# A graph layer's edge counts in 7 places a dense tile instead of 11, three lists to a PSUM bank

## The chip, the cores and the metric

The kernel runs on one core of one Trainium2 chip. The metric is the device time of one execution in microseconds; the time before is the median of three runs, 1500.9 us (1500.37 to 1501.51).

## The reference

6250 nodes of 256 numbers, 200000 edges. Three branches read the normalised input: a graph convolution, a mixer (linear attention with two layer norms and a gelu network), and, on the sum of the two, a mixture of eight experts with a capacity of tokens each.

```python
xn = layernorm(x)
# graph convolution, self loops added
h = xn @ W;  norm = dinv[src] * dinv[dst]
gnn = relu(segment_sum(h[src] * norm[:, None], dst) + b)
# mixer: q, k = elu(.) + 1; linear attention over all nodes, 8 heads
t  = (q @ kv) / (q @ ksum + 1e-6)
x1 = layer_norm(t + xn, ln1_g, ln1_b)
mix = layer_norm(gelu(x1 @ W1.T + b1) @ W2.T + b2 + x1, ln2_g, ln2_b)
x = x + gnn + mix
# experts: gate, argmax, place in the expert's buffer, two layers, times the probability
idx = argmax(softmax(layernorm(x) @ gate_w + gate_b))
x = x + ffn_of_experts(layernorm(x), idx)
```

The edges are sorted by their destination `dst`.

## The kernel before

The nodes are 49 tiles of 128. A first stage (to about 247 us) normalises x, makes q, k and v, sums the attention's `kv`, and leaves the rows `h` of all nodes twice: in SBUF as `tab` and in DRAM as `g_dram`. The stage that is changed follows, to about 1130 us. The experts run behind it, to the end.

**Dense tiles.** 32 of the 49 destination tiles (`ND = 32`) get their sum as a full product: a matrix A of edge counts (source node by destination node) times `tab`, 49 products of 128x128 by 128x512 into the bank `ps_d` (L1199), after an identity product (L1195, the self loops) and a product with left-over rows (L1196). A is counted by TensorE: the edges of a tile's 128 destinations are cut into 44 lists (`NG`), 40 of three destinations and 4 of two. Of each list VectorE makes two one-hot matrices (`onehots`, L1134): `lo` (128 wide, the source within its tile) and `hi` (148 wide, source tile times destination in the list). Their product, `lo` by `hi` (L1177), is 49 x 3 = 147 columns of counts. Two lists share a PSUM bank `bp` (pool of 2); ScalarE evicts it as uint8 into `A` (L1181; L1184 for the two-node lists). Later ScalarE widens `A`, 4 or 5 of the 49 blocks at a time, to `A_r` (L1165, 2 buffers), the weights of the products at L1199.

`dense()` is a generator that yields once a place; a tile has `half = NG // 4` = 11 places. In place p the tile u−1 gets the products of share p (places 1 to 10), the one-hots of place p+1 are made (`lo` and `hi` in 3 buffers), the next share is widened, and `counted` issues the counts of place p−1 with their evictions: four lists, two banks. In place 0 there are no products of L1199. In the last place `put_sum` (ScalarE, L1121) and `put_rest` (VectorE, L1126) take `ps_d` away.

**Gathered tiles.** The other 17 tiles are summed over gathered rows: 33 products each (`EB`), 561 in all (`NGT`). For each, GpSimd starts an indirect DMA of 128 rows into `gt` (L1230; 9 buffers, 7 ahead), VectorE makes a one-hot `oh` for every two (L1245, made four products ahead, 3 buffers), TensorE multiplies into `ps` (L1256). Each tile has an identity product first and, two products later, one with `ohg` (L1255; `ohg` from L1242). `gather()` yields after each product.

**Rounds.** Everything else of the 49 tiles goes by pairs: 25 rounds. A step of a round is a function, and `at(k, f)` puts it into place k of a plan; round a starts at `SLOTS_A_ROUND * a`, 14 places. In the order of a round: `scaled`, `attend` (two halves, L1453, a bank each) and `attended` (VectorE, L1464 and L1466), `mix_stats`, `mix_norm` (L1379), `mix_turn` and `mix_turned` (L1488), `first` (L1496), `gelu` (ScalarE, two instructions, L1504), `second` (L1512, L1514), `mixed` (L1523); second statistics, `gain`, `shift`, `joined`; then for an earlier pair `add_bias`, `to_slot` (L1390), statistics, `slot_turn`, `slot_turned`, `gate` (L1422), `put_logits` (L1427), and for every two pairs a `routing` that is walked in ten steps and ends in scatters to `xbuf` (GpSimd, L1337). `start_roots` and `end_roots` make the inverse roots of a round's variances on VectorE. All PSUM banks of the rounds come from one pool of three (`bank()`, tile `mm`).

The engines run their own instructions in the order in which this driver issues them:

```python
g_rate = (NGT + LAG - 0.8 * ahead) / (n_dense - G_EARLY - ahead)
...
for n in range(n_dense + 1):
    ...
    step("d")
    while counts["s"] < min(s_end, (n - S_LATE) * S_RATE) and step("s"):
        pass
    while counts["g"] < 0.8 * min(n + 1, ahead) + max(0, n + 1 - ahead) * g_rate and step("g"):
        pass
```

So one place is: the dense tile's share, one place of the plan of rounds (`S_RATE` = 1.0104), and about 1.6 gathered products.

## Time and profile before

| | |
|---|---|
| median of 3 runs | 1500.9 us (1500.37 to 1501.51) |
| profiled execution, its own time | 1500.01 us |
| its span | 1498.2 us |
| mean granted TensorE clock | 0.979 |
| first stage (0 to 247 us), TensorE busy | 215.75 us |
| dense, gathered and rounds (247 to 1130 us), TensorE busy | 845.85 of 883 us |
| the end of the rounds (1130 to 1190 us), TensorE busy | 50.32 of 60 us |
| experts (1190 us to the end), TensorE busy | 285.75 of 308 us |

PE is TensorE's matrix products and PEld its weight loads, DVE is VectorE, ACT ScalarE, POOL GpSimd, SP the engine that only starts DMAs. A group of instructions is shown by its line and operation, with the tiles it writes and reads (`out<-in`), its number, its busy time and the mean of one in ns, and the idle time of its engine just before it with what ended that. A wait is shown as the line that waited, the line that it waited for, the sum in us, how often, and the longest.

### The profile page before, as it was taken

What the parts mean: (1) busy time and instruction counts of PE and PEld (TensorE: products, weight loads), DVE (VectorE), ACT (ScalarE), POOL (GpSimd) and SP (SyncE); (2) the same over time, 40 slices, a digit from 0 to 9 for tenths busy, and PEclk for the clock granted to TensorE, in tenths of its full rate; (3) what the DMA queues carried; (4) which work ended last, traced back from release to release, by engine and by line L of the source; (5) the groups of instructions that cost most, each with busy time, mean ns of one, the idle gap of its engine ahead of it and who ended that gap; (6) DMA issues with size and microseconds to landing.
All of it is one profiled execution on the core that took longest, in us unless ns stands there. A gap on an engine that the chain in (4) does not pass through costs nothing. (4 is left out here: it accounts for less than half of the span.)

```text
span 1498.2 us, 22383 instructions
## 1 busy us (share of the span) xinstructions
PE 1397.7 (93%) x7002; PEld 1020.9 (68%) x7002; DVE 1004.2 (67%) x3435; ACT 900.1 (60%) x2051; POOL 745.3 (50%) x725
## 2 busy tenths in 40 slices
PE   5998997999998999999999989999997999999996
PEld 2665664777776777777776767767775767766854
DVE  6787696678887887878888878888865322222322
ACT  2776564677776777677776767777674333333321
POOL 0101542777776677777766677777661201111111
PEclk9999998999999999999999999999998999999998
DMA  8438675877787777877777777777765343333130
GB/s 266 144 124 275 195 233 172 225 198 201 188 219 207 180 201 211 223 200 214 204 202 205 196 192 202 186 209 210 182 170 171 120 149 110 127 129 132 47 109 11
DMA packets 173459, 267.52 MB, mean 179 GB/s; under 512 B 26409, under 2 KB 73984, under 8 KB 173318
## 3 DMA queue, kind: packets, MB, share of 16 engines
q0 software_dynamic: 89168, 166.39, 42.7%
q1 hardware_dynamic: 83268, 98.39, 19.9%
q10 hardware_dynamic: 882, 1.05, 0.3%
q8 instruction: 65, 1.06, 0.3%
q14 instruction: 76, 0.62, 0.1%
HBM read 208.05 MB, written 60.39 MB: 179 GB/s over the span
## 5 line engine op out<-in xcount | busy, mean ns | idle before, releaser
L1230 POOL DMA_INDIRECT gt<-g_dram,idxc x561 | 592.9, 1057 | 217.1 <-PE ps L1256 79.7
L1199 PE MATMUL ps_d<-tab,A_r 128*128 128x512 f32 x1568 | 425.8, 401 | 10.2 <-ACT A_r L1165 9.9
L1199 PEld LDWEIGHTS ps_d<-tab,A_r 128*128 128x128 f32 x1568 | 292.7, 190 | 88.6 <-ACT A_r L1165 26.5
L1181 ACT CAST A<-bp 128x294 uint8<-128x294 f32 x640 | 237.2, 430 | 186.9 <-PE bp L1177 185.4
L1165 ACT CAST A_r<-A 128x640 fp32r<-128x640 uint8 (+1 forms) x320 | 230.7, 723 | 6.6 <-PE ps_d L1199 5.0
L1256 PE MATMUL ps<-gt,oh 128*128 128x512 f32 x561 | 220.4, 451 | 2.5 <-DVE oh L1245 2.5
L1177 PE MATMUL bp<-hi,lo 128*128 128x147 bf16 x1408 | 187.3, 264 | 22.0 <-DVE hi L1134 13.1
L1177 PEld LDWEIGHTS <-lo 128*128 128x128 bf16 x1408 | 105.0, 105 | 123.0 <-issue 49.3
L1838 POOL DMA_INDIRECT out<-rep,who x43 | 42.5, 989 | 279.4 <-DVE rep L1835 225.5
L1804 PE MATMUL hpf<-xet,w1e 128*128 128x128 f32 (+3 forms) x576 | 159.2, 434 | 8.2 <-ACTq L1916 3.5
L1134 DVE TENSOR_TENSOR lo<-rowb,two 128x512 bf16<-128x512 bf16 x352 | 147.4, 419 | 21.0 <-PE bp L1177 13.6
L1134 DVE TENSOR_TENSOR hi<-hib,two 128x592 bf16<-128x592 bf16 x352 | 161.5, 459 | 0.0
L1814 PE MATMUL ypf<-w2e,hm 128*128 128x256 f32 (+1 forms) x688 | 151.4, 379 | 0.0
L1814 PEld LDWEIGHTS ypf<-w2e,hm 128*128 128x128 f32 (+1 forms) x688 | 128.8, 188 | 21.6 <-issue 2.6
L1245 DVE TENSOR_TENSOR oh<-rowb,rel 128x256 fp32r<-128x256 bf16 x281 | 116.2, 414 | 40.8 <-PE ps L1256 40.2
L1804 PEld LDWEIGHTS hpf<-xet,w1e 128*128 128x128 f32 x576 | 92.6, 198 | 66.4 <-issue 55.7
L1806 ACT ACTIVATE hm<-hpf,fb_s 128x128 f32<-128x128 f32 (+3 forms) x144 | 72.3, 513 | 87.6 <-PE hpf L1804 84.8
L1816 DVE TENSOR_TENSOR y<-ypf,fb_s 128x256 f32<-128x256 f32 (+1 forms) x43 | 18.2, 423 | 130.6 <-PE ypf L1814 130.6
L1256 PEld LDWEIGHTS ps<-gt,oh 128*128 128x128 f32 x561 | 97.2, 195 | 7.9 <-DVE oh L1245 3.4
L1817 ACT ACTIVATE y<-y,xe 128x256 f32<-128x256 f32 (+1 forms) x43 | 21.8, 508 | 124.8 <-DVE y L1816 124.8
L892 PE MATMUL mm<-wqkv_s,xnt 128*128 128x512 f32 (+1 forms) x196 | 93.4, 599 | 0.3 <-DVE tab L481 0.3
L1337 POOL DMA_INDIRECT xbuf<-slot,put x46 | 48.0, 1044 | 58.2 <-issue 29.5
(376 smaller groups left out, 1993.3 us busy)
## 6 DMA issues: line engine op xcount, KB each, us to landing
g_dram<-tab SPq DMA_DIRECT2D x24, 512.0 KB
xbuf<-zeros SPq DMA_DIRECT2D x26, 384.0 KB
gt<-g_dram,idxc POOLq DMA_INDIRECT x561, 3.8
w1e<-in_fw SPq DMA_DIRECT2D x8, 1024.0 KB
w2e<-in_fw SPq DMA_DIRECT2D x8, 1024.0 KB
xe<-xbuf SPq DMA_DIRECT2D x7, 1028.0 KB
xt<-in_x SPq DMA_DIRECT2D x28, 256.0 KB
xe<-xbuf SPq DMA_DIRECT2D x9, 771.0 KB
```

The lines of the kernel that those rows point to most:

```text
L892: nc.tensor.matmul(kp[:r, :], xnt[:, c, i * r:i * r + r], wqkv_s[:, c, D:3 * D], start=(c == 0), stop=(c == 1))
L1134: V.tensor_tensor(one.rearrange("p g (w t) -> p g w t", t=2), row.rearrange("p (w t) -> p w t", t=2).unsqueeze(1).to_broadcast([P, 4, w // ...
L1165: nc.scalar.copy(o[:, :s1 - s0, :], mats[u][:, s0:s1, :])
L1177: nc.tensor.matmul(both[:, :, h * GN:(h + 1) * GN], lo[:, 2 * i + h, :], hi[:, 2 * i + h, :NB * GN].rearrange("p (s k) -> p s k", k=GN), s ...
L1181: nc.scalar.copy(mats[uu][:, :, GN * g:GN * (g + 2)], both)
L1199: nc.tensor.matmul(acc_ps, A[:, hi - s0, :], source(hi), start=False, stop=(hi == NB - 1))
L1230: nc.gpsimd.indirect_dma_start(out=gt, out_offset=None, in_=g_dram, in_offset=bass.IndirectOffsetOnAxis(ap=idxs[j // P][:, j % P:j % P + 1 ...
L1245: V.tensor_tensor(oh, rowb.unsqueeze(1).to_broadcast([P, 2, P]), rel[:, m:m + 2].unsqueeze(2).to_broadcast([P, 2, P]), op=OP.is_equal)
L1256: nc.tensor.matmul(ps, ohs.pop(i), tiles.pop(i), start=False, stop=(e == EB - 1))
L1804: nc.tensor.matmul(hp[:, :nn], w1e[:, c, f * P:(f + 1) * P], xet[:, c, at:at + nn], start=(c == 0), stop=(c == 1))
L1806: nc.scalar.activation(hm[:, f, :nn], hp[:, :nn], AF.Relu, bias=fb1_s[:, e * 8 + f:e * 8 + f + 1])
L1814: nc.tensor.matmul(yp[:r, :], hm[:, f, (i - i0) * P:(i - i0) * P + r], w2e[:, f, :], start=(f == 0), stop=(f == FF - 1))
```

## The change

A dense tile has 7 places (`PLACES`) instead of 11. Places 0 to 5 count six lists, the last one eight: six and the last two of two-node lists, with two more. Three lists share a bank (441 columns, one eviction); in the last place a bank holds two lists of three nodes and two of two (two evictions). Two-node lists are counted on 98 columns. `lo` and `hi` are made for six lists at once, in 2 buffers instead of 3. The 49 blocks are widened in 12 shares (`CHUNKS`), 11 of four and one of five, two of which are multiplied in each of places 1 to 6; both are widened in the place before, still in 2 buffers. Rounds take 9 places instead of 14, every step has a new place (the gate goes from step 1 of the next round, beside gelu and without attend, to step 2, with gelu and attend's second half), and the routing is walked at other offsets. About 2.3 gathered products follow in a place, and about 4.1 in place 0 of a tile (`g_due`). The tail's table is numbered anew.

```diff
-SLOTS_A_ROUND = 14
-S_RATE = 1.0104
-S_LATE = 6
-G_EARLY = 8
+PLACES = 7
+CHUNKS = 12
+SLOTS_A_ROUND = 9
+S_RATE = 1.022
+S_LATE = 4
+G_EARLY = 5
+G_FIRST = 1.6
...
-                one = de.tile([P, 4, w], BF16, name=name, tag=name, bufs=3)
...
+                for g0, n, tag in ((6 * p, 6, name), (6 * PLACES, NG - 6 * PLACES, name + "2"))[:1 + (p == PLACES - 1)]:
+                    one = de.tile([P, n, w], BF16, name=name, tag=tag, bufs=2 if n == 6 else 1)
...
+        def banks_of(p):
+
+            g = 6 * p
+            if p < PLACES - 1:
+                return [[(g, 3)], [(g + 3, 3)]]
+            return [[(g, 2), (NL, 2)], [(g + 2, 2), (NL + 2, 2)]]
...
-            def share(p):
-                return (p - 1) * NB // (half - 1), p * NB // (half - 1)
+            def share(c):
+                return c * NB // CHUNKS, (c + 1) * NB // CHUNKS
...
-                    for i in range(2):
-                        g = 4 * pp + 2 * i
+                    for runs in banks_of(pp):
                         bp = bps.tile([P, 512], F32, name="bp", tag="bp")
...
+                            for g in range(g0, g0 + n):
+                                nc.tensor.matmul(both[:, :, at:at + w], lo[g],
+                                                 hi[g][:, :NB * GN].rearrange("p (s k) -> p s k", k=GN)[:, :, :w],
+                                                 start=True, stop=True)
...
-                        A, (s0, s1) = parts.pop(p), share(p)
...
+                        for c in (2 * p - 2, 2 * p - 1):
+                            A, (s0, s1) = parts.pop(c), share(c)
...
-                        widened(u - 1, p + 1)
+                        widened(u - 1, 2 * p)
+                        widened(u - 1, 2 * p + 1)
...
-                at(k + 4, attend, a, 1)
+                at(k + 2, attend, a, 1)
...
-                at(k + 1, gelu, a)
+                at(k + 2, gelu, a)
...
-                at(k + 15, gate, c)
...
+                for d, f in zip((6, 7, 8, 9) if end else (7, 9, 10, 11), (slot_norm, slot_turn, slot_turned, gate)):
+                    at(k + d, f, c, *([4] if f is slot_norm else []))
...
-        g_rate = (NGT + LAG - 0.8 * ahead) / (n_dense - G_EARLY - ahead)
+        g_start = 1.25
+        g_rate = (NGT + LAG - g_start * ahead) / (n_dense - G_EARLY - ahead)
+
+        def g_due(n):
+            if n < ahead:
+                return g_start * (n + 1)
+            u, p = divmod(n - ahead, PLACES)
+            return g_start * ahead + g_rate * (PLACES * u + G_FIRST + p * (PLACES - G_FIRST) / (PLACES - 1))
...
-            while counts["g"] < 0.8 * min(n + 1, ahead) + max(0, n + 1 - ahead) * g_rate and step("g"):
+            while counts["g"] < g_due(n) and step("g"):
```

More of the change, by code (lines that the diff above doesn't have):

```diff
@@ L1132, in onehots @@
             for h, (name, row, w) in enumerate((("lo", rowb, P), ("hi", hib, HW))):
-                one = de.tile([P, 4, w], BF16, name=name, tag=name, bufs=3)
-                V.tensor_tensor(one.rearrange("p g (w t) -> p g w t", t=2),
-                                row.rearrange("p (w t) -> p w t", t=2).unsqueeze(1).to_broadcast([P, 4, w // 2, 2]),
-                                lists[:, h, 4 * p:4 * p + 4, :].unsqueeze(2).to_broadcast([P, 4, w // 2, 2]),
-                                op=OP.is_equal)
-                o.append(one)
-            return o
+                ones_of = {}
+                for g0, n, tag in ((6 * p, 6, name), (6 * PLACES, NG - 6 * PLACES, name + "2"))[:1 + (p == PLACES - 1)]:
+                    one = de.tile([P, n, w], BF16, name=name, tag=tag, bufs=2 if n == 6 else 1)
+                    V.tensor_tensor(one.rearrange("p g (w t) -> p g w t", t=2),
+                                    row.rearrange("p (w t) -> p w t", t=2).unsqueeze(1).to_broadcast([P, n, w // 2, 2]),
+                                    lists[:, h, g0:g0 + n, :].unsqueeze(2).to_broadcast([P, n, w // 2, 2]),
+                                    op=OP.is_equal)
+                    for g in range(n):
+                        ones_of[g0 + g] = one[:, g, :]
+                o.append(ones_of)
+            return o
+        def banks_of(p):
[3 more added lines that the diff above has]
+            return [[(g, 2), (NL, 2)], [(g + 2, 2), (NL + 2, 2)]]
         def twice(u):
@@ L1155, in dense, with widened @@
             acc_ps = ohl = None
-            half = NG // 4
-            def share(p):
-                return (p - 1) * NB // (half - 1), p * NB // (half - 1)
-            def widened(u, p):
-                s0, s1 = share(p)
-                o = parts[p] = de.tile([P, 5, P], FR, name="A_r", tag="A_r")
+            half = PLACES
+            def share(c):
+                return c * NB // CHUNKS, (c + 1) * NB // CHUNKS
+            def widened(u, c):
+                s0, s1 = share(c)
+                o = parts[c] = de.tile([P, 5, P], FR, name="A_r", tag="A_r")
                 nc.scalar.copy(o[:, :s1 - s0, :], mats[u][:, s0:s1, :])
@@ L1171, in counted @@
                     uu, pp, (lo, hi) = made.pop(0)
-                    for i in range(2):
-                        g = 4 * pp + 2 * i
+                    for runs in banks_of(pp):
                         bp = bps.tile([P, 512], F32, name="bp", tag="bp")
-                        both = bp[:, :2 * NB * GN].rearrange("p (s k) -> p s k", k=2 * GN)
-                        for h in range(2):
-                            nc.tensor.matmul(both[:, :, h * GN:(h + 1) * GN], lo[:, 2 * i + h, :],
-                                             hi[:, 2 * i + h, :NB * GN].rearrange("p (s k) -> p s k", k=GN),
-                                             start=True, stop=True)
-                        if g < NL:
-                            nc.scalar.copy(mats[uu][:, :, GN * g:GN * (g + 2)], both)
-                        else:
-                            at = GN * NL + 2 * (g - NL)
-                            nc.scalar.copy(mats[uu][:, :, at:at + 4].rearrange("p s (g k) -> p s g k", g=2),
-                                           both.rearrange("p s (g k) -> p s g k", g=2)[:, :, :, :2])
+                        k = sum(n * (GN if g < NL else GN - 1) for g, n in runs)
+                        both = bp[:, :NB * k].rearrange("p (s k) -> p s k", k=k)
+                        at = 0
+                        for g0, n in runs:
+                            w = GN if g0 < NL else GN - 1
+                            for g in range(g0, g0 + n):
+                                nc.tensor.matmul(both[:, :, at:at + w], lo[g],
+                                                 hi[g][:, :NB * GN].rearrange("p (s k) -> p s k", k=GN)[:, :, :w],
+                                                 start=True, stop=True)
+                                at += w
+                        at = 0
+                        for g0, n in runs:
+                            w = GN if g0 < NL else GN - 1
+                            to = GN * g0 if g0 < NL else GN * NL + w * (g0 - NL)
+                            nc.scalar.copy(mats[uu][:, :, to:to + w * n], both[:, :, at:at + w * n])
+                            at += w * n
             for u in range(ND + 1):
@@ L1196, in dense @@
                             nc.tensor.matmul(acc_ps, ohl, left, start=False, stop=False)
-                        A, (s0, s1) = parts.pop(p), share(p)
-                        for hi in range(s0, s1):
-                            nc.tensor.matmul(acc_ps, A[:, hi - s0, :], source(hi), start=False, stop=(hi == NB - 1))
+                        for c in (2 * p - 2, 2 * p - 1):
+                            A, (s0, s1) = parts.pop(c), share(c)
+                            for hi in range(s0, s1):
+                                nc.tensor.matmul(acc_ps, A[:, hi - s0, :], source(hi), start=False, stop=(hi == NB - 1))
                     if u < ND:
@@ L1210, in dense @@
                     if u >= 1 and 0 < p < half - 1:
-                        widened(u - 1, p + 1)
-                    if u < ND and p == half - 3:
+                        widened(u - 1, 2 * p)
+                        widened(u - 1, 2 * p + 1)
+                    if u < ND and p == half - 2:
                         ohl = de.tile([P, P], FR, name="ohl", tag="ohl", bufs=1)
@@ L1220, in dense @@
                     if u >= 1 and p == 0:
+                        widened(u - 1, 0)
                         widened(u - 1, 1)
@@ L1556, in rounds @@
             for a in range(NGR):
-                k = S_ * a - (2 if a == NGR - 1 else 0)
-                at(k - 9 if a else 0, load, a)
-                at(k + 2, scaled, a)
-                at(k + 2, attend, a, 0)
-                at(k + 4, attend, a, 1)
-                at(k + 3, attended, a, 0)
-                at(k + 5, attended, a, 1)
-                at(k + 7, mix_stats, a, 0)
-                at(k + 10, mix_norm, a, 0, (0, 1))
-                at(k + 12, mix_turn, a)
-                at(k + 13, mix_turned, a)
-                at(k + 13, gained, a)
-                k += S_
-                at(k, first, a)
-                at(k + 1, gelu, a)
+                e = int(a == NGR - 1)
+                k = S_ * a - e
+                at(k - 6 if a else 0, load, a)
+                at(k + 1, scaled, a)
+                at(k, attend, a, 0)
+                at(k + 2, attend, a, 1)
+                at(k + 2, attended, a, 0)
+                at(k + 3, attended, a, 1)
+                at(k + 4, mix_stats, a, 0)
+                at(k + 6, mix_norm, a, 0, (0, 1))
+                at(k + 7, mix_turn, a)
+                at(k + 8, mix_turned, a)
+                at(k + 8, gained, a)
+                k += S_ - (e or a == NGR - 2)
+                at(k + 1, first, a)
+                at(k + 2, gelu, a)
                 at(k + 3, second, a)
@@ L1575, in rounds @@
                     break
-                at(k + (5 if a == NGR - 2 else 6), mix_stats, a, 2)
-                at(k + 11, mix_norm, a, 2, (0, 1))
-                at(k + 11, shift, a)
-                at(k + 13, gain, a)
-                at(k + 14, joined, a)
+                at(k + 4, mix_stats, a, 2)
+                at(k + 8, mix_norm, a, 2, (0, 1))
+                at(k + 8, shift, a)
+                at(k + 9, gain, a)
+                at(k + 9, joined, a)
             for c, r in takes.items():
-                k = S_ * r - (2 if c == TAILC - 1 else 0)
-                needs[k - 2] = c
-                at(k - 2, add_bias, c)
+                end = c == TAILC - 1
+                k = S_ * r - end
+                needs[k - 1] = c
+                at(k - 1, add_bias, c)
                 at(k + 1, to_slot, c)
                 at(k + 2, slot_stats, c, 4)
-                at(k + 12, slot_norm, c, 4)
-                at(k + 13, slot_turn, c)
-                at(k + 14, slot_turned, c)
-                at(k + 15, gate, c)
+                for d, f in zip((6, 7, 8, 9) if end else (7, 9, 10, 11), (slot_norm, slot_turn, slot_turned, gate)):
+                    at(k + d, f, c, *([4] if f is slot_norm else []))
                 if c % 2 == 0:
@@ L1598, in put_logits @@
                     logits(c, b[0], 2 * (c % 2))
-                at(k + 16, put_logits)
+                at(k + (10 if end else 12), put_logits)
                 if c % 2:
@@ L1605, in begin @@
                         walk(b[1])
-                    at(k + 17, begin)
-                    soon = (18, 19, 19, 21, 21, 22, 23, 23, 24, 24)
-                    sooner = (18, 22, 23, 24, 25, 26, 27, 27, 28, 28)
-                    for d in soon if c == TAILC - 1 else sooner if c == TAILC - 3 else (18, 24, 25, 27, 28, 29, 30, 30, 31, 32):
+                    at(k + (11 if end else 13), begin)
+                    soon = (11, 12, 13, 14, 15, 15, 15, 15, 16, 16)
+                    for d in soon if end else (13, 15, 16, 17, 18, 18, 19, 19, 20, 20):
                         at(k + d, lambda c=c: walk(batches[c - 1][1]))
             for r in range(NGR):
-                at(S_ * r + (6 if r == NGR - 1 else 8), start_roots)
-                at(S_ * r + (7 if r == NGR - 1 else 9), end_roots)
+                e = int(r == NGR - 1)
+                at(S_ * r + 4 - e, start_roots)
+                at(S_ * r + 5 - e, end_roots)
             def to_sum(c, first):
@@ L1674, in rounds @@
             last = b2
-            needs[z + 15], needs[z + 17], needs[z + 25] = b1, b0, b2
+            needs[z + 10], needs[z + 11], needs[z + 16] = b1, b0, b2
             for k, f, *args in (
-                    (10, enough),
-                    (15, add_bias, b1), (15, to_sum, b1, 4),
-                    (16, mix_stats, last, 2), (17, add_bias, b0), (17, to_sum, b0, 0),
-                    (18, start_roots), (19, end_roots),
-                    (20, mix_norm, last, 2, (0, 1)), (20, filled, b1, 4), (21, filled, b0, 0),
-                    (22, stored, b1), (22, stored, b0), (22, tail_lists, b0),
-                    (22, gain, last), (22, shift, last), (22, joined, last),
-                    (25, lead, 3), (25, add_bias, b2), (25, to_sum, b2, 0), (25, stored, b2), (25, all_roots),
-                    (25, slot_turn, b1), (25, slot_turned, b1), (25, slot_turn, b0), (25, lead), (25, slot_turned, b0),
-                    (25, gate, b1), (25, gate, b0), (25, tail_logits, b0, b0, 0), (25, tail_logits, b1, b0, 2),
-                    (25, tail_routing, b0, [b0, b1]), (25, go, b0, 2),
-                    (26, filled, b2, 0), (26, lead), (26, slot_turn, b2), (26, slot_turned, b2),
-                    (26, go, b0, 3), (26, lead), (26, gate, b2),
-                    (27, tail_lists, b2), (27, tail_logits, b2, b2, 0), (27, tail_routing, b2, [b2]), (27, go, b2, 2),
-                    (27, go, b0, 6), (27, lead), (28, go, b2, 2), (28, lead, 2), (28, go, b2, 2), (28, told),
-                    (28, go, b2, 20), (28, lead, 30)):
@@ new lines, in rounds @@
+                    (6, enough),
+                    (10, add_bias, b1), (10, to_sum, b1, 4),
+                    (11, mix_stats, last, 2), (11, add_bias, b0), (11, to_sum, b0, 0),
+                    (12, start_roots), (13, end_roots),
+                    (14, mix_norm, last, 2, (0, 1)), (14, filled, b1, 4), (14, filled, b0, 0),
+                    (15, stored, b1), (15, stored, b0), (15, tail_lists, b0),
+                    (15, gain, last), (15, shift, last), (15, joined, last),
+                    (16, lead, 3), (16, add_bias, b2), (16, to_sum, b2, 0), (16, stored, b2), (16, all_roots),
@@ new lines, in rounds @@
+                    (16, slot_turn, b1), (16, slot_turned, b1), (16, slot_turn, b0), (16, lead), (16, slot_turned, b0),
+                    (16, gate, b1), (16, gate, b0), (16, tail_logits, b0, b0, 0), (16, tail_logits, b1, b0, 2),
+                    (16, tail_routing, b0, [b0, b1]), (16, go, b0, 2),
+                    (17, filled, b2, 0), (17, lead), (17, slot_turn, b2), (17, slot_turned, b2),
+                    (17, go, b0, 3), (17, lead), (17, gate, b2),
+                    (18, tail_lists, b2), (18, tail_logits, b2, b2, 0), (18, tail_routing, b2, [b2]), (18, go, b2, 2),
@@ L1693, in rounds @@
+                    (18, go, b0, 6), (18, lead), (19, go, b2, 2), (19, lead, 2), (19, go, b2, 2), (19, told),
+                    (19, go, b2, 20), (19, lead, 30)):
                 at(z + k, f, *args)
@@ L1704, in graph_block_kernel @@
         G, Dn, S = gather(), dense(), rounds()
-        n_dense = (ND + 1) * (NG // 4)
-        ahead = NG // 4
+        n_dense = (ND + 1) * PLACES
+        ahead = PLACES
         counts = {"g": 0, "d": 0, "s": 0}
@@ L1718, in step @@
             return False
-        g_rate = (NGT + LAG - 0.8 * ahead) / (n_dense - G_EARLY - ahead)
-        s_end = SLOTS_A_ROUND * (len(twos) - 1) + 25
+        g_start = 1.25
[5 more added lines that the diff above has]
+            return g_start * ahead + g_rate * (PLACES * u + G_FIRST + p * (PLACES - G_FIRST) / (PLACES - 1))
+        s_end = SLOTS_A_ROUND * (len(twos) - 1) + 16
         begun, early_in = [], False
```

## Prediction

> **What bounds the kernel now.** I read the page's busy shares first, then the same by windows, because the page's share is a mean over three different stages. The stage that the change touches runs from about 250 to 1130 us.

> ```profile
> PE 1397.7 (93%) x7002; PEld 1020.9 (68%) x7002; DVE 1004.2 (67%) x3435; ACT 900.1 (60%) x2051; POOL 745.3 (50%) x725
> ```

> ```profile
> 280.00:1100.00 820.00, 785.62 (x4321) 586.32 (x4319) 656.88 (x2197) 594.23 (x1338) 597.41 (x564) 0.99 0.77 201
> 821.00:824.40 3.40, 3.40 (x12) 2.49 (x11) 3.26 (x12) 0.81 (x3) 1.96 (x2) 0.50 0.87 225
> ```

> The columns are stretch, length, busy time of PE, PEld, DVE, ACT, POOL, granted clock, DMA share and GB/s. In the 820 us PE idles 34.4 us; the next engine, DVE, idles 163. PE is the bound, in order, and what delays its head instruction is paid in full. POOL is nearer than it looks: 597.4 us busy, and 0.30 us before each of 564 indirect DMAs, is 767 of 820.

> The identity product, one a dense tile, is the yardstick:

> ```profile
> L1195 PE MATMUL ps_d<-tab,ident x32: 394/478/776, 261.2 to 1124.0; 128*128 128x512 f32 x32
> ```

> (1124.0 − 261.2) / 31 = 27.83 us a tile. On the same scale POOL needs 767 / 820 × 27.83 = 26.0. The waits of PE, same window (total, times, longest):

> ```profile
> PE ps_d L1199 <- ACT A_r L1165: 9.2, 13, 1.6
> PE ps L1255 <- DVE ohg L1242: 6.7, 5, 2.8
> PE bp L1177 <- DVE hi L1134: 5.1, 7, 1.3
> PE bp L1177 <- ACT A L1184: 5.1, 7, 1.1
> PE ps L1256 <- DVE oh L1245: 2.5, 3, 1.2
> PE bp L1177 <- ACT A L1181: 2.0, 7, 0.3
> ```

> Most belong to the tile change, where no accumulating products are due: the counts follow close on each other and wait for their own evictions. The gate (L1422) is not in the list:

> ```profile
> L1422 PE MATMUL mm<-gate_s,xmt x168: 170/256/257, 381.6 to 1094.5; 128*128 128x8 f32 x168
> its engine sat idle before it (us, times) until:
> who waited for it (us, times):
> ```

> Nothing stands under "sat idle": PE never waited at the gate.

> **The change, part by part.** Prices of PE come from its timeline, as distances of starts:

> ```profile
> 599.89 1.32 PE L1199 MATMUL ps_d<-tab,A_r 128*128 128x512 f32 x5
> 601.05 0.51 PE L1177 MATMUL bp<-hi,lo 128*128 128x147 bf16 x4
> 601.39 0.65 PE L1453 MATMUL mm<-kvb,q 128*128 128x132 f32 x4
> ```

> Five accumulating products take 1.16 us (0.232 each), four counts 0.34 (0.085 each). A gathered product takes 0.235, but 0.31 as the first after counts: a group of counts costs about 0.08 beside itself.

> *Fewer groups of counts.* 7 instead of 11 a tile saves 4 × 0.08 = 0.32 us. The four two-node lists count 98 columns instead of 147, about 0.02 each, 0.08. On PE, the bound, 32 × 0.40 = **−13 us**. The counts themselves, the 49 products and the 561 gathered ones stay.

> *Evictions and widenings.* ACT's rows:

> ```profile
> L1181 ACT CAST A<-bp 128x294 uint8<-128x294 f32 x584 | 216.0, 430 | 173.1 <-PE bp L1177 171.9
> L1165 ACT CAST A_r<-A 128x512 fp32r<-128x512 uint8 x30 | 18.6, 619 | 1.0
> L1184 ACT CAST A<-bp 128x196 uint8<-128x196 f32 x60 | 16.9, 331 | 8.3 <-PE bp L1177 7.2
> L1504 ACT ACT_TABLE_LOAD x11 | 14.1, 1283 | 0.2
> ```

> 430 ns for 294 columns and 331 for 196 is 1.0 ns a column; 441 columns would take 0.58 us. A tile goes from 20 × 0.430 + 2 × 0.331 = 9.26 to 12 × 0.58 + 2 × 0.43 + 2 × 0.33 = 8.5. Eleven widenings of 0.619 and one of 0.735 make 7.5 instead of 7.2. ACT has 226 us to spare: nothing. The one-hots on DVE, two instructions of 0.419 and 0.459 in each of 11 places, become 7 of about 0.55 and 0.61 and two small ones: 9.7 to 8.7 us a tile, in sum nothing either. It is the spacing that matters: all work beside the dense tile now comes in fewer, larger pieces.

> *The tile change.* Place 0 of a tile now has about 4.1 gathered products instead of 1.6, 2.5 × 0.235 = 0.6 us more cover for evictions and first widenings. It can take away at most 9.2 + 5.1 + 5.1 + 2.0 = 21 us of waits, and at least nothing. The last place packs 8 lists where it had 4, so I take **−18**.

> *The gate's bank: a wait that is new.* Rounds share three PSUM banks. When step 2 of a nine-step round begins, attend's first half still holds one until attended (DVE) and first another until gelu (ACT); both readers are issued in this same step. Attend's second half takes the third, and the gate, now in this step too, must take one that is being read. The order of the built programs agrees: of 20 gates in the stage 13 wait for gelu's second instruction and 7 for attended. From the end of that place's products ACT has a widening, two evictions and two gelus to go, 0.62 + 2 × 0.58 + 2 × 0.48 = 2.74 us, and 1.283 more with a table load (11 loads for 24 gelus in the window). PE has six counts and attend's four records of 0.112: 0.96. So 1.8 or 3.05 us, mean 2.4, unless ACT is ahead there (0). Behind the gate stand the place's gathered products and the next place's accumulating ones: all of PE. I take 13 × 2.4 and 7 × 0.5 for those on DVE: **+35** (bounds 0 and 20 × 2.4 = 48).

> *DVE in lumps.* Step 4 now has mixed (0.69), four statistics (2.4) and a start of the roots (0.85) beside one-hots (1.15) and a gathered one-hot (0.41): 5.5 us in one place, where PE has 8 × 0.232 + 6 × 0.085 + 2.3 × 0.235 and two switches, 3.1. (0.85 is five small operations of 0.17.) With lo and hi in two buffers instead of three DVE cannot run further ahead, and a gathered one-hot is made four products, now 1.6 places, before its use. The excess of 2.4 us a round is lost at most, nothing at least, over 24 rounds; nearest is the wait for oh, 2.5 us in all in the trace, so the low end: 0.6 a round, **+15**.

> *The clock.* After a long wait PE runs slow, once at 820 us:

> ```profile
> 820.36 0.50 PE L1255 MATMUL ps<-left,ohg 128*128 128x512 f32 x1 [2.02 <-DVE ohg L1242]
> ...
> 820.93 2.27 PE L1199 MATMUL ps_d<-tab,A_r 128*128 128x512 f32 x5
> ```

> 2.02 us idle, and the window row 821.00:824.40 shows the clock at 0.50: 1.7 us lost. The 2.78 us wait on the same product at 454 us did the same; waits of 1.0 to 1.6 us mostly did not. Seven new waits of some 3 us, one for each gate behind a table load, make 7 × 1.7 = **+12** (bounds 0, and 20 × 1.7 = 34 if every gate trips it).

> [...]

> *Moved rounds.* Nine places of about 3.9 us last as long as fourteen of 2.5, so rounds end with the dense tiles as before. The scatter to xbuf, for which DVE's slot waits 51.4 us in the window, is one step nearer to its reader; DVE's reserve of 163 us hides that, and without it a wait of at most 9 us (the longest seen) would show once or twice. Nothing.

> **Sum.** The profiled execution took 1500.0 us (span 1498.2), 0.9 below the median of 1500.9. 1500 − 13 − 18 + 35 + 15 + 12 = **1531**; left in words, 31 us won and 62 lost.

> **Rivals.** *Faster: the gate waits for nothing.* ACT reaches the place early, because it has 226 us of reserve and place 0's extra products let it catch up; gelu is read before PE is through with attend. For it: before, gelu sat in the gate's place as well. Against it: then the bank was not gelu's, and the second widening of a place can't begin before the place's first four products are done, since A_r has two buffers. It gives 1500 − 13 − 21 = 1466; a tile would take 26.8 us, above POOL's 26.0, which would hold at 1500 − 32 × 1.83 = 1441. It decides if gate, DVE and clock together cost under 31 us, that is under 1.3 us a round.

> *Much slower: DVE is late every round.* Every gate waits 2.4, the gathered one-hot 1.7 in every round, and each round trips the clock once: 1500 − 31 + 48 + 24 × 1.7 + 20 × 1.7 = 1592. DVE's own row speaks for it (80% busy on the mean, so far above where the lump is), its small wait so far against.

> *It doesn't do what it says, or cancels.* A scheduler could have kept the old order; the built order shows seven groups of counts a tile and rounds of nine steps, so this is only the case in which new waits replace old ones one for one: 1500.

> **How the numbers follow.** The forecast's case, 1505 to 1565 around 1531, has 0.40; the slowest, 1565 to 1620, 0.22; the faster one, 1441 to 1495, 0.34; no difference 0.04. A measurement of this kernel can tell about 0.2%, 3 us, from no change: slower 0.62, same 0.04, faster 0.34. The range leaves out a tenth at each end: 1462 to 1592. Of the slower cases alone it would be 1508 to 1592.

> **What would show it.** If right: distance of identity products about 28.8 us; PE waits "mm <- ht (gelu)" at the gate, 13 or more, 1.5 to 3 us each; waits for A and hi at the tile change nearly gone; more slices at clock 0.50. If the gate has no idle before it and identity products stand 26.8 us apart, the first rival holds; if the waits are for oh or ohg on DVE, the second. The forecast is wrong altogether if the stage after 1130 us moves, which I leave at its length.

## The result, and the profile after

The changed kernel takes 1630.1 us (median of 4 runs, 1628.4 to 1634.9) against 1501.2: a ratio of 1.086 (95% interval 1.084 to 1.089), 129 us slower. A second set of runs gave 1629.3 us, again 1.086. Slower was forecast, but 1531 us; the range ended at 1592.

The page's busy shares of the profiled execution (span 1628.8 us), then the stage from the first identity product of a dense tile to the last, first of after and then of before. The columns are stretch, length, busy time of PE, PEld, DVE, ACT and POOL, granted clock, DMA share and GB/s.

```profile
PE 1441.9 (89%) x7002; PEld 1076.8 (66%) x7002; DVE 1001.8 (62%) x3243; ACT 909.5 (56%) x1923; POOL 729.9 (45%) x725
```

```profile
264.00:1260.00 996.00, 872.77 (x4560) 673.95 (x4559) 684.50 (x2110) 634.95 (x1286) 611.72 (x593) 0.93 0.66 174
```

```profile
261.00:1124.00 863.00, 828.62 (x4563) 619.02 (x4563) 685.51 (x2290) 625.27 (x1410) 625.61 (x593) 0.99 0.77 201
```

The same 31 tiles take 133 us more. PE idles 123 instead of 34 us, and is busy 44 us longer with as many products, at a mean clock of 0.93 instead of 0.99. DVE has as much work as before, and ACT 10 us more: no other engine has become the bound. The yardstick of the prediction:

```profile
L1213 PE MATMUL ps_d<-tab,ident x32: 393/481/776, 264.3 to 1260.3; 128*128 128x512 f32 x32
```

(1260.3 − 264.3) / 31 is 32.1 us a tile, where 27.8 were needed and 28.8 forecast. The waits of PE in the stage, 264 to 1260 us (total, times, longest; the expectations below quote 280 to 1200 us, where the first line is 35.4, 20, 4.2 and the second to fourth are the same):

```profile
PE ps L1277 <- DVE oh L1266: 40.8, 21, 5.4
PE mm L1443 <- ACT ht L1525: 26.1, 13, 3.8
PE mm L1443 <- DVE s L1487: 21.5, 7, 4.9
PE ps L1276 <- DVE ohg L1263: 17.3, 7, 3.7
PE ps_d L1218 <- ACT A_r L1179: 6.0, 4, 2.0
```

The gate (L1443) waits 20 times, 13 for gelu and 7 for attended, as the order of the programs had it. Larger, 58.1 us where the forecast had 15, are the waits for the one-hots of the gathered products (`oh`, L1266, and `ohg`, L1263); in the kernel before they were 9.2 us. One such wait in PE's timeline, and the clock in the windows around it:

```profile
729.48 1.88 PE L1443 MATMUL mm<-gate_s,xmt 128*128 128x8 f32 x8 [3.81 <-ACT ht L1525]
731.21 2.05 PE L1277 MATMUL ps<-gt,oh 128*128 128x512 f32 x4
```

```profile
729.50:736.30 6.80, 6.80 (x24) 5.62 (x25) 6.38 (x20) 1.15 (x2) 5.34 (x5) 0.51 0.97 282
736.30:740.00 3.70, 3.70 (x17) 2.49 (x16) 0.82 (x3) 1.24 (x2) 2.82 (x3) 1.00 0.92 256
```

After 3.81 us of waiting PE runs at half the clock for 6.8 us, twice the stretch that the prediction had seen. So each execution can be split in three, for the stage from the first identity product to the last: what PE idles; half of its busy time in stretches at clock 0.50, as an estimate of what the clock cost (in the changed kernel's stage an accumulating product took 0.427 us at clock 0.50 and 0.234 at 1.00, medians of 87 and 1233 distances of starts, so half is a little high); and the rest, the work at full clock.

| execution | stage us | idle | stretches at 0.50 | lost to the clock | rest |
|---|---|---|---|---|---|
| before | 862.8 | 34.4 | 4 | 6.8 | 821.6 |
| after | 996.0 | 123.2 | 25 | 63.3 | 809.4 |
| difference | +133.2 | +88.8 | +21 | +56.5 | −12.2 |

In three of the five later groups of runs the kernel before itself took 1598 to 1612 us, with idle time on PE, DVE and ACT that the trace puts down to no instruction of the kernel (in one of them 35, 52 and 111 us in this stage; at most 3 us in the same kernel elsewhere); of those groups, marked below, only the ratio to the kernel before is read.

### The profile page after: what moved, and what is told of

It reads as the page before. It is cut to its first block, busy times and chain, and to the rows that moved or that the text cites. A ratio compares the mean times of both kernels' runs of the same rounds, so it can differ in the third digit from the quotient of the medians.

```text
span 1628.8 us, 22430 instructions
## 1 busy us (share of the span) xinstructions
PE 1441.9 (89%) x7002; PEld 1076.8 (66%) x7002; DVE 1001.8 (62%) x3243; ACT 909.5 (56%) x1923; POOL 729.9 (45%) x725
## 5 line engine op out<-in xcount | busy, mean ns | idle before, releaser
L1251 POOL DMA_INDIRECT gt<-g_dram,idxc x561 | 574.8, 1025 | 344.3 <-PE ps L1277 210.1
L1218 PE MATMUL ps_d<-tab,A_r 128*128 128x512 f32 x1568 | 418.5, 411 | 6.0 <-ACT A_r L1179 6.0
L1218 PEld LDWEIGHTS ps_d<-tab,A_r 128*128 128x128 f32 x1568 | 310.2, 198 | 84.5 <-ACT A_r L1179 9.1
L1179 ACT CAST A_r<-A 128x512 fp32r<-128x512 uint8 (+1 forms) x384 | 234.4, 628 | 215.0 <-PE ps_d L1218 213.0
L1202 ACT CAST A<-bp 128x441 uint8<-128x441 f32 (+2 forms) x512 | 237.0, 529 | 69.2 <-PE bp L1194 68.0
L1139 DVE TENSOR_TENSOR lo<-rowb,two 128x768 bf16<-128x768 bf16 (+1 forms) x256 | 131.0, 522 | 212.5 <-PE bp L1194 198.4
L1277 PE MATMUL ps<-gt,oh 128*128 128x512 f32 x561 | 210.1, 462 | 42.4 <-DVE oh L1266 40.8
L1194 PE MATMUL bp<-hi,lo 128*128 128x147 bf16 (+1 forms) x1408 | 168.5, 271 | 9.8 <-DVE hi L1139 8.6
L1194 PEld LDWEIGHTS <-lo 128*128 128x128 bf16 x1408 | 115.4, 112 | 77.9 <-issue 55.7
L1139 DVE TENSOR_TENSOR hi<-hib,two 128x888 bf16<-128x888 bf16 (+1 forms) x256 | 145.1, 577 | 0.0
L1266 DVE TENSOR_TENSOR oh<-rowb,rel 128x256 fp32r<-128x256 bf16 x281 | 113.8, 418 | 32.4 <-PE ps L1277 32.1
```

The costliest lines, as they stand in the source:

```text
L1139: V.tensor_tensor(one.rearrange("p g (w t) -> p g w t", t=2), row.rearrange("p (w t) -> p w t", t=2).unsqueeze(1).to_broadcast([P, n, w // ...
L1179: nc.scalar.copy(o[:, :s1 - s0, :], mats[u][:, s0:s1, :])
L1194: nc.tensor.matmul(both[:, :, at:at + w], lo[g], hi[g][:, :NB * GN].rearrange("p (s k) -> p s k", k=GN)[:, :, :w], start=True, stop=True)
L1202: nc.scalar.copy(mats[uu][:, :, to:to + w * n], both[:, :, at:at + w * n])
L1218: nc.tensor.matmul(acc_ps, A[:, hi - s0, :], source(hi), start=False, stop=(hi == NB - 1))
L1251: nc.gpsimd.indirect_dma_start(out=gt, out_offset=None, in_=g_dram, in_offset=bass.IndirectOffsetOnAxis(ap=idxs[j // P][:, j % P:j % P + 1 ...
```

## The experiments

Times are medians.

**Which part does it.** First the two halves by themselves: the changed dense tiles with the old plan of rounds, and the old dense tiles with the changed plan.

```diff
 # dense7_rounds14: after, with the plan and the tail table of before
-SLOTS_A_ROUND = 9
-S_RATE = 1.022
+SLOTS_A_ROUND = 14
+S_RATE = 1.5877
 # dense11_rounds9: before, with the plan and the tail table of after
-SLOTS_A_ROUND = 14
-S_RATE = 1.0104
+SLOTS_A_ROUND = 9
+S_RATE = 0.6504
```

> The changed kernel's dense tiles and gathered products (7 places, banks of three lists, two buffers of one-hots, more products in place 0) with the plan of rounds of the kernel before: 14 steps a round and its own tail table, 1.588 steps a place so that rounds take as long. Theory (the plan of nine steps does the harm): dense tiles alone are a gain, 1470 to 1500, with no wait at the gate. Rival (larger pieces and two buffers in the dense tile do the harm): 1560 to 1620, oh and ohg waits as in the changed kernel.

> The kernel before with the changed kernel's plan of rounds alone: 9 steps a round at 0.650 steps a place; dense tiles and gathered products as before. Theory (the plan of nine steps does the harm): gate waits stay, about 1 to 2 us each as ACT has less before gelu in a place, DVE's lump of step 4 is carried by three buffers: 1530 to 1570. Rival (the dense tile does the harm): 1495 to 1510.

1603.2 us (ratio 1.066, 1.064 to 1.069) and 1569.9 us (1.045, 1.043 to 1.046), beside 1503.2. Each number lies in the range of the explanation that blames the half in question, the second at its very edge; so neither half is to blame alone: both do harm. The waits of the first and of the second, 262 to 1260 us:

```profile
PE ps L1277 <- DVE oh L1266: 43.9, 25, 5.2
PE ps L1276 <- DVE ohg L1263: 20.7, 8, 7.1
PE mm L1517 <- ACT x1t L1509: 17.9, 12, 2.2
PE mm L298 <- ACT slot L1400: 14.3, 21, 2.2
```

```profile
PE mm L1422 <- DVE s L1466: 29.4, 11, 5.0
PE ps_d L1199 <- ACT A_r L1165: 28.3, 29, 2.9
PE ps L1255 <- DVE ohg L1242: 4.5, 3, 3.0
...
PE ps L1256 <- DVE oh L1245: 2.2, 2, 1.5
```

The waits for oh and ohg go with the dense tile of 7 places, under either plan; the gate's waits go with the plan of nine steps, with either dense tile. But with 11 places they are nearly all for attended (29.4 us) and not for gelu (3.8), where the expectation had gelu. Each half also has waits that the changed kernel has not: the first 32 us for x1t and slot, probably since 1.6 steps fall into one place there, the second 28 us for A_r, where the kernel before had 9.2; so the halves' +100 and +67 are not to be added up to +129.

**The gate's bank.** One step later for the gate and the logits behind it:

```diff
-                for d, f in zip((6, 7, 8, 9) if end else (7, 9, 10, 11), (slot_norm, slot_turn, slot_turned, gate)):
+                for d, f in zip((6, 7, 8, 9) if end else (7, 9, 10, 12), (slot_norm, slot_turn, slot_turned, gate)):
...
-                at(k + (10 if end else 12), put_logits)
+                at(k + (10 if end else 13), put_logits)
```

> The changed kernel with the gate and put_logits one step later (12 and 13 instead of 11 and 12); nothing else. The changed kernel's trace shows 20 waits of the gate, 47.6 us (26.1 for gelu, 21.5 for attended on DVE), and ten of its slow stretches of the clock begin at them. Theory (each wait costs itself and trips the clock): the gate waits nowhere, 47.6 us and about 10 x 3 us of clock go: 1545 to 1565. Rival (DVE is late anyway, behind the slot's wait for the scatters, and only the place of the wait changes): the part for attended turns up at oh, ohg or the next product of the rounds, 1590 to 1610.

1591.8 us, ratio 1.059 (1.054 to 1.063), 38 us less than the changed kernel. The gate waits no more, yet (the third line is DVE's):

```profile
PE ps L1277 <- DVE oh L1266: 57.0, 26, 5.4
PE ps L1276 <- DVE ohg L1263: 19.0, 9, 4.0
...
DVE lo L1139 <- PE bp L1194: 161.2, 88, 8.3
```

Of 47.6 us at the gate 18 came back at oh and ohg, 76.0 instead of 58.1. The rival's number came true, and the theory's cause too: the place that the plan gives the gate makes its wait, but DVE is late on its own.

**Why attended is late.** DVE's waits in the changed kernel, 264 to 1260 us:

```profile
DVE lo L1139 <- PE bp L1194: 197.6, 101, 6.5
DVE slot L1411 <- issue: 32.2, 8, 4.9
...
DVE slot L1411 <- DMA xbuf<-slot,put: 10.0, 2, 5.3
```

The second and third lines are to_slot. Around 804 us DVE ends `hi`, stands 4.93 us at L1411, and the two scatters of the buffer that it needs were started by POOL at 803.3 and 805.05 us, in the same place; attended is behind it, and the gate then waits 4.91 us:

```profile
805.05 1.01 POOL L1358 DMA_INDIRECT xbuf<-slot,put  x1 [0.30 <-ACT s L1466]
808.78 0.17 DVE L1411 CAST slot<-pid 128x2 int32<-128x2 f32 x1 [4.93 <-issue]
```

So to_slot was moved behind attended:

```diff
-                at(k + 1, to_slot, c)
-                at(k + 2, slot_stats, c, 4)
+                at(k + (1 if end else 3), to_slot, c)
+                at(k + (2 if end else 3), slot_stats, c, 4)
```

> The changed kernel with to_slot and slot_stats in step 3 instead of 1 and 2; nothing else. In the changed kernel's trace DVE stands 36.9 us at to_slot (9 times), waiting for scatters that were issued in the same or the place before, and attended, which is behind it, is what seven gates wait for (21.5 us, 3 us each). Theory: with attended's first half ahead of to_slot the seven waits fall to about 1 us and five slow stretches of the clock go: 1590 to 1605. Rival (attended is late because of DVE's own load): no change, 1625 to 1635.

1606.6 us (1.069, 1.065 to 1.072), 23 us less, just above the theory's range. DVE's wait at to_slot fell from 42 to 5 us, and the longest wait of the gate for attended from 4.9 to 2.0; but there are nine of them now, 17.6 us instead of 21.5. So the scatter made them long, and without it DVE still comes late. More was won where the edit did not aim: the gate's waits for gelu fell from 26.1 us to 12.2, for a reason that no run shows.

**Why oh is late.** The first line above is the answer to test. DVE took its instructions in the order of issue: in the case above PE was through with attend at 807.3 us, and attended began at 810.79, behind the to_slot that stood. In place p DVE was given the one-hots of place p+1, which need the buffer whose counts are issued in the same place p; DVE stands there 197.6 us (190.8 between 280 and 1200 us; 13.5 in the kernel before, with three buffers), and everything behind, oh above all, would then start when PE is already near it. A third buffer with 7 places was not tried; instead the one-hots are issued one place later, when the counts of their buffer are a place old (late_gate_b has this and the gate's edit):

```diff
-            made.append((0, 0, onehots(two, 0)))
...
-                        if p < half - 1:
-                            made.append((u, p + 1, onehots(two, p + 1)))
-                        elif u + 1 < ND:
+                        made.append((u, p, onehots(two, p)))
+                        if p == half - 1 and u + 1 < ND:
                             two = two2
-                            made.append((u + 1, 0, onehots(two, 0)))
```

> The changed kernel with one-hots made one place later and the gate one step later. Theory (buffers of the one-hots hold DVE): against the gate alone (1591.8 us, oh and ohg 76 us) those waits fall to about 20 us, slow stretches of the clock from 23 to about 12: 1520 to 1545. Rival (DVE's load): 1575 to 1600.

1518.2 us (1.011, 1.009 to 1.013), a little under the theory's range and far from the rival's. With the gate moved in both, this edit alone is worth 1591.8 − 1518.2 = 74 us. Oh waits 28.6 instead of 57.0 us, ohg 8.0 instead of 19.0. DVE's waits, 264 to 1144 us, are now mostly those of an engine that has caught up with PE:

```profile
DVE oh L1263 <- PE ps L1274: 73.2, 44, 4.5
DVE ag L1129 <- ACT ag L1124: 40.2, 29, 3.6
DVE slot L1408 <- issue: 28.8, 7, 5.5
...
DVE lo L1139 <- PE bp L1193: 4.2, 7, 1.1
```

The wait at lo fell from 161.2 to 4.2 us, with DVE's work as it was: so it was the wait for the buffers, more than the load, that made oh late. The same kernel, in a marked group:

> The same with the gate one step later too. Theory: both groups of waits gone, idle time of PE about 40 us as before and the clock's loss about 10 us: 1500 to 1520. Rival (DVE's load): 1575 to 1600.

Ratio 1.001 (0.998 to 1.004). And the one-hots alone, with the gate left, twice in marked groups:

> The changed kernel with the one-hots of a place made one place later: lo and hi of place p are issued to DVE in place p (counted in place p+1), not in place p-1. With two buffers lo then waits for counts of the place before, not of this place. Theory (DVE stands 190 us at lo for the counts, and oh and ohg stand behind it in its order): the waits for oh and ohg, 52.7 us, fall under 15, slow stretches of the clock from 25 to about 12: 1560 to 1585; the gate's 47.6 us stay. Rival (DVE's own load of step 4 makes oh late, not the buffers): oh and ohg stay over 40 us, and hi is late on top: 1625 to 1650.

> The changed kernel with the one-hots made one place later and the gate left where it is; with the changed kernel, the gate alone (1591.8) and both (1518.2) this completes a square. If the two causes add: 1629 - (1592 - 1518) = 1555. If each wait hides part of the other: nearer 1590.

Ratios 1.014 (1.008 to 1.021) and 1.018 (1.013 to 1.024); in the first, oh and ohg waited 13.2 and 5.6 us. Beside the 1.001 of late_gate in the same group the gate's share is then about 1.4%; whether the two causes add in the usual surrounding stays open.

**All repairs together.** Besides one-hots and gate, to_slot as above, and DVE's lump of step 4 spread:

```diff
-                at(k + 4, mix_stats, a, 0)
+                at(k + 3, mix_stats, a, 0)
...
-                at(S_ * r + 4 - e, start_roots)
+                at(S_ * r + 5 - 2 * e, start_roots)
```

> The same with to_slot in step 3, the mixer's first statistics in step 3 and the roots in step 5. Theory: 1500 to 1530, a little under the one without it, since the buffers were what held DVE. Rival (DVE's lump of step 4 matters by itself): 30 us or more under it.

1503.9 us, ratio 1.001 (0.9999 to 1.002): level with the kernel before, and 14 us under late_gate_b. That is less than the 30 that the rival, DVE's lump, asked for. The waits left over, 262 to 1250 us:

```profile
PE ps L1274 <- DVE oh L1263: 13.7, 8, 5.4
PE ps L1274 <- DMA gt<-g_dram,idxc: 11.0, 10, 3.2
PE ps L1273 <- DVE ohg L1260: 5.1, 4, 2.4
```

In the marked group:

> The same, and to_slot and its statistics in step 3, the mixer's first statistics in step 3, the roots in step 5: DVE's lump of step 4 falls from 5.5 to about 3.5 us. Theory: 1480 to 1505, with waits for oh nearly gone. Rival (DVE's load): here too the lump is smaller, so 1540 to 1570, clearly under the run without it.

Ratio 1.003 (0.999 to 1.007).

**The tile change.** The uneven gathered products alone, in the kernel before (the old 0.8 a place kept for the first tile):

```diff
+G_FIRST = 2.5
...
+            u, p = divmod(n - ahead, 11)
+            return 0.8 * ahead + g_rate * (11 * u + G_FIRST + p * (11 - G_FIRST) / 10)
```

> The kernel before with 4.1 gathered products in place 0 of a tile and less in the others. Theory (they cover the waits of the tile change): waits for A and hi nearly gone there, 1485 to 1495. Rival (missed in the other places): A_r waits grow, 1500 to 1515.

1517.5 us, ratio 1.011 (1.008 to 1.014): 15 us slower. Neither expectation had what happened:

```profile
PE ps L1257 <- DVE oh L1246: 24.1, 19, 5.4
PE ps L1256 <- DVE ohg L1243: 4.4, 3, 3.8
...
PE bp L1178 <- ACT A L1182: 3.2, 11, 0.3
...
PE ps_d L1200 <- ACT A_r L1166: 2.0, 7, 0.6
```

The waits for A and A_r did go, from 16 to 6 us, and that for hi (5.1) altogether. But oh is made four products ahead, and four products are now one place: its wait rose from 2.5 to 24.1. In a marked group:

> The kernel before with the uneven gathered products alone: place 0 of a tile gets the worth of 2.5 places (4.1 products), the other ten less. Theory (they cover the waits of the tile change): the waits for A and hi there, 12 us, nearly go: 1485 to 1495. Rival (the products are missed in the other places, where they stand between counts and the next products, and widening is waited for there): A_r waits grow, 1500 to 1515.

Ratio 1.016 (1.009 to 1.022). The reverse, even products in the changed and in the repaired kernel, fell into marked groups each time:

> The changed kernel with gathered products spread evenly (G_FIRST 1.0: about 2.6 in every place). In the kernel before, 4.1 products in place 0 alone cost 15 us, since the wait for oh rose from 2.5 to 24 us. Theory (a one-hot made four products ahead is too late where one place takes four): oh waits at the tile change fall by 10 to 20 us of 35, waits for A, hi or A_r of some 10 us come instead: 1605 to 1625. Rival (the buffers of lo and hi alone make oh late): no gain, 1630 to 1650 since the cover of the tile change is gone.

> The changed kernel with gathered products spread evenly, again, for the same reason. Theory (part of the oh waits is the uneven products'): 1605 to 1625, oh 15 to 25 us. Rival (the buffers alone): 1630 to 1650.

> The version with one-hots late, gate, to_slot, statistics and roots moved (1503.9, same as before) with gathered products spread evenly. Theory as in the first: oh (13.7 us), waits for gt (11.0) and ohg (5.1) nearly gone, waits for A at the tile change up by 10 to 20: 1490 to 1503. Rival (cover of the tile change is worth more): 1505 to 1520.

> The same with G_FIRST 1.3, about 3.3 products in place 0: between the two, 1488 to 1502, the best of the three if both kinds of wait grow faster than in proportion.

> One-hots late, gate, to_slot, statistics and roots moved, and G_FIRST 1.3, again, since its last run fell where the kernel before took 1611.8 us (ratio 0.996 there). Theory (uneven products make oh and gt late, even ones uncover the tile change; a middle is best): 1488 to 1500 where the kernel before takes 1502. Rival (what is won at oh is lost at the tile change): 1500 to 1507.

After_even had ratios of 1.041 (1.035 to 1.047) and 1.051 (1.045 to 1.057), with oh at 16.7 and 16.9 us in the stage and 20 and 23 us more at the same product behind other work of DVE; the changed kernel has no run in those groups, so what its uneven products cost stays open. The repaired kernel with even products had 0.999 (0.995 to 1.002), with G_FIRST 1.3 first 0.996 (0.994 to 0.999), then 0.999 (0.996 to 1.003). No version is shown to beat the kernel before.

> The changed kernel unchanged, beside the three that follow, since the last four kernels ran where the kernel before took 1600.6 us and its engines stood still without a cause in the trace. If this is the usual surrounding: 1625 to 1635 and a ratio of 1.086. If it is the slower one: the ratio says how much of the changed kernel's loss is left there; with the disturbance felt by all alike, 1.08.

That is the second set of the first section: 1629.3 us. The split of the stage for the unmarked kernels (the profiled execution of late_gate_b took 1523.3 us, that of late_gate_slot_lumps_b 1498.5, where the medians are 1518.2 and 1503.9):

| execution | stage us | idle | stretches at 0.50 | lost to the clock | rest |
|---|---|---|---|---|---|
| dense7_rounds14 | 969.0 | 115.1 | 20 | 37.3 | 816.6 |
| dense11_rounds9 | 927.2 | 76.0 | 13 | 27.6 | 823.6 |
| gate_later | 955.3 | 101.4 | 23 | 46.5 | 807.4 |
| slot_later | 975.8 | 113.3 | 23 | 50.3 | 812.3 |
| late_gate_b | 879.2 | 53.1 | 7 | 18.9 | 807.1 |
| late_gate_slot_lumps_b | 859.5 | 40.1 | 5 | 10.3 | 809.1 |
| before_gfirst_b | 872.9 | 39.9 | 5 | 9.5 | 823.4 |

But for dense7_rounds14 (115.1 us idle, 37.3 lost), the loss to the clock falls with the idle time through all of them, from 63.3 us on 123.2 in the changed kernel to 6.8 on 34.4 in the kernel before. The last repair still has 12 us less work than the kernel before, but 6 us more idle time and 3 to 4 us more for the clock.

## Why the prediction was wrong, step by step

*Fewer groups of counts, −13.* Right in size: the rest fell by 12.2 us, and in every kernel with 7 places it lies at 807 to 817, in those with 11 at 822 to 824. The 817 belongs to the old plan of rounds, where only 5 us went; so part of the 12 may not be the groups'.

*Evictions, widenings, one-hots in sum: nothing.* Right in sum (DVE 684.5 us against 685.5 in the stage); wrong for the order. The text took it that two buffers keep DVE from running ahead, and priced only its lump; that DVE is then held at `lo`, 101 times and 197.6 us in all, with oh behind it, was not seen.

*DVE in lumps, +15, at most 58.* Among the waits the step that failed most: oh and ohg wait 58.1 us instead of 9.2, +48.9. It was taken near the low end by the row for oh, 2.5 us, which belongs to a kernel with three buffers. And the cause was mostly another: not the lump of step 4 but the wait at `lo`. With that wait taken away oh and ohg fell from 76.0 to 36.6 us (gate_later to late_gate_b, 74 us of time); spreading the lump and moving to_slot then took them to 18.8 (14 us of time).

*The gate, +35, at most 48.* The mechanism and the 20 places were right, the size 47.6. The 13 for gelu were 2.0 us on the mean where 2.4 were taken; the 7 for attended 3.1 where 0.5 were. That the sum, 47.6, came out at the upper bound of 48 is in part luck, since the bound had 2.4 for each. The second term was mis-sized, at least in part because of the next step.

*Moved rounds: nothing.* Wrong. The scatter one step nearer to its reader was put down to DVE's reserve; but a reserve on the mean is none for what stands behind the wait in order, and attended, then the gate, stood behind it. slot_later puts 23 us on it, with the waits for gelu in them.

*The tile change, −18.* The waits there did fall, from 21.4 to 6.0 us. That the same four products come faster than their one-hots are made was not in the sum; in the kernel before the waits for oh rose by it from 2.5 to 24.1 us, and this alone turned the gain into a loss of 15.

*The clock, +12, at most 34.* Wrong by the largest amount: +56.5. The bound counted gates alone and 1.7 us for each; there were 21 stretches more, and 17 of the 25 are 6.8 us long, that is up to 3.4 us of loss by the same half. The row of 2.02 us that the prediction went by held: behind waits of 2.0 to 2.5 us the clock fell in 38 of 52 cases (last section).

With the measured terms the idle time is nearly accounted for: 47.6 at the gate, 48.9 at oh and ohg and −15.4 at the tile change are 81 of the 88.8 us. With 56.5 for the clock and −12.2 of work that is 133 us in the stage; in the two profiled executions 3 us more ahead of it and 6 less behind it leave 131, and the medians differ by 129. Of the rivals the second was the nearest: DVE late, waits tripping the clock. It lay 38 us short, 22 of them by the clock (34 against 56.5). The first, the gate that waits for nothing, is out: it waited 20 times, and even with the gate moved the kernel took 1592.

## What to carry to other kernels

Before a pipeline is cut into fewer, larger pieces, go through each engine's instructions in their order and ask what stands behind the one that now waits for its buffer: in the changed kernel no wait of PE's in the stage is for the counting one-hots themselves, and yet taking DVE's wait for their buffers away was worth 74 us, by what stood behind it. A busy share of two thirds (DVE, 684.5 of 996 us) says nothing of that. Price a new wait on TensorE with what the clock adds to it (here 56.5 us on 88.8), and a lead given in products (four ahead) in time: when the products were bunched, the waits behind it rose from 2.5 to 24.1 us.

## What the runs showed of the hardware

All figures here are counted in the profiled executions of this case, from the granted clock and PE's instructions in the stage. Over the ten unmarked ones (before, after twice, and the seven of the last table), TensorE's waits that began at full clock, by length, and how many had a stretch at clock 0.50 begin during them or within 3.5 us behind them; then the same in the first profiled executions of before and after alone:

| wait, us | waits, ten executions | with a stretch at 0.50 | waits, before and after | with a stretch at 0.50 |
|---|---|---|---|---|
| 1.0 to 1.5 | 102 | 21 | 22 | 4 |
| 1.5 to 2.0 | 56 | 16 | 7 | 2 |
| 2.0 to 2.5 | 52 | 38 | 10 | 7 |
| 2.5 to 3.0 | 20 | 17 | 3 | 3 |
| 3.0 to 3.5 | 11 | 10 | 1 | 1 |
| over 3.5 | 55 | 55 | 13 | 13 |

In these runs, then, the clock fell behind 21 of 102 waits of 1.0 to 1.5 us and behind all 55 over 3.5. The stretches of the stage lasted 3.41 us, all four of before and 8 of the 25 of after, or 6.83 us, the other 17 of after. In these two, the stretch was one of 3.41 us for 7 of the 13 waits under 2.5 us that had one, and of 6.83 us for all 13 over 3.5; in the ten it was 6.8 us for 34 of the 55 over 3.5.

Waits of like length went both ways. Two of the changed kernel, for the same one-hots, and the clock behind each:

```profile
912.61 0.50 PE L1277 MATMUL ps<-gt,oh 128*128 128x512 f32 x1 [2.17 <-DVE oh L1266]
1123.01 0.50 PE L1277 MATMUL ps<-gt,oh 128*128 128x512 f32 x1 [2.26 <-DVE oh L1266]
```

```profile
913.71:917.12 3.41, 3.41 (x13) 2.59 (x12) 1.77 (x9) 1.73 (x4) 0.67 (x1) 0.50 0.54 143
1120.74:1127.00 6.26, 4.00 (x23) 3.01 (x23) 5.85 (x27) 3.85 (x10) 3.40 (x4) 1.00 0.68 170
```

| idle in a cell at full clock, us | cells | followed by 0.50 |
|---|---|---|
| under 0.75 | 426 | 0 |
| 0.75 to 2.0 | 50 | 8 |
| over 2.0 | 21 | 21 |

A stretch ended behind 29 of the 36 cells at 0.50 with under 0.75 us of idle time, and behind none of the 10 with more. Of the two waits above, the one of 2.17 us lies in one cell, and the one of 2.26 us has 1.18 us in one and 1.09 in the next. Between 0.75 and 2.0 us the cells overlap: the most idle time without a fall is 1.70 us, the least with one 1.20. Why some of these cells were followed by 0.50 and others not stays open.
